# First convolution in nine block products, row sums by DMA, PSUM in pairs of banks

## The chip, the cores and the metric

The kernel runs on one core of a Trainium2 chip. The core has TensorE (PE; matmuls, with weight loads as PEld), VectorE (DVE), ScalarE (ACT) and GpSimd (POOL), and SyncE (SP), which here only issues DMAs. Each engine takes its instructions in order from its own queue. The metric is the device time of one execution in microseconds. The kernel before takes 885.22 us, the median of three runs (883.51 to 889.34).

## The reference

There are B = 4 images, C = 64 channels, and each (image, channel) is a 256 x 256 matrix, float32. Cut to what matters:

```python
# layer 0: per channel a separable filter k = hx (outer) hy, made by two small sine networks
k_f = rfft2(k, s=(512, 512)) / 512
u_f = rfft2(x, s=(512, 512))
y = irfft2(u_f * k_f, s=(512, 512))[..., :256, :256]     # a causal 2-D convolution
x = y + x * bias[:, None, None]
# layer 1
scores = einsum('bpsd,bptd->bpst', x, x) / sqrt(256)     # Gram matrix of the rows
red = sum(scores * weights[None], axis=-1, keepdims=True)
y = x + red                                              # one number per row s
y_hat = (y - mean) * rsqrt(var + 1e-5)                   # over images and positions, per channel
out = y_hat * gamma + beta
```

Because the filter is separable, the 2-D convolution is two products with lower triangular Toeplitz matrices of 256 x 256, one per side of the image.

## The kernel before

Each channel is worked on as a whole. Its four images lie as two pairs: u picks the half of the partitions (64 rows of the array) and v the other index. A 256 x 256 matrix is cut into blocks of 64, so that four 64 x 64 matmuls, t = 0 to 3, run beside each other on the four quarters of the array.

**TensorE, per channel, three stages.** `conv_x0` is the second convolution (from z, the result of the first, to x0); `conv_z` (lines 197 to 216) is the first convolution of the *next* channel; `gram` is the Gram matrix of x0. A Toeplitz matrix that is lower triangular has ten non-zero blocks out of sixteen, so a convolution has, for each of its four output block columns, products over 4, 3, 2 and 1 blocks: four matmuls with 256, 192, 128 and 64 moving columns. `gram` uses the symmetry and also has ten blocks.

**Around the stages.** `copy_z` (ScalarE) takes the first convolution out of PSUM, reversed. `add_bias` (VectorE, line 246) adds x times bias to the second one and writes x0. `weigh` (VectorE) multiplies the Gram blocks with the weights: two products with an accumulator give row sums (`red0`, lines 328), one product gives `pr` (line 319), whose columns are still to be summed over the partitions. `spread` (line 340) places the row sums on a diagonal and adds them to `pr`, giving `sp`. `all_sum` (GpSimd, line 348) sums `sp` over the partitions into `rd`, and `pick_red` (ScalarE, line 357) copies the second image's half. `add_red` (line 364) adds this to x0 and accumulates the sum for the mean; a small all-reduce on GpSimd (line 368) adds over partitions. `minus_mean` (line 411), `squares` (line 416), `sum_squares` (line 422, GpSimd), `root` (lines 428 to 432) and the Newton steps with scale and shift (lines 437 to 450, VectorE) make the normalisation, and `finish` (line 462, ScalarE) writes the output tile, which SP stores (line 463).

**Tables.** The filter values of all channels are written once to `g_dram`, four copies. `load_h` (line 188) loads a channel's Toeplitz rows into `toep` in four DMAs of 16 partitions, and `copy_h` (line 193, ScalarE) doubles them onto the other 64 partitions.

**The order** is written by hand: the program runs under a manual schedule, so each engine's queue, SP's and GpSimd's among them, has its instructions in the order in which the main loop writes them. One pass of that loop, for channel c, works on several channels at once: convolution and Gram of c, first convolution of c+1, loads for c+2 and c+3, row sums of p = c-1, mean and squares of q = c-2, scale and outputs of f = c-3 and e = c-4. The last two channels have their own code, `last_channels`, in which the row sums go through TensorE (`red_by_pe`). PSUM is used in eight single banks.

Of the kernel before, what the change touches and what calls it, by code (L numbers as in the profile page):

```python
# [16 lines left out]
P = 128  # L17
EMB = 33
FFT = 2 * S
GW = S + P // 2  # L20
COPIES = 4
H = P // 2
# [15 lines left out]
def conv_scores_bn_kernel(  # L38
# [29 lines left out]
    def load_xt(c, v, n):  # L68
        if not n:
            xts[c, v] = ld.tile([P, 4, S], F32, tag=f"xt{v}", name=f"xt_{c}_{v}", bufs=4)  # L70
        part = bass.ts(n, 2)
        nc.sync.dma_start(xts[c, v][:, part], xT[c, v, :, part])
# [39 lines left out]
    g_sb = const.tile([P, GW], F32, name="g_sb")  # L112
    nc.vector.memset(g_sb[:, S:], 0.0)

    g0_sb = const.tile([P, 2, GW], F32, name="g0_sb")
# [3 lines left out]

    g_dram = dram.tile([COPIES, C, 2, GW], F32, name="g_dram")  # L120

    hs[0] = ld.tile([P, 2, GW], F32, tag="toep", name="toep_0")
    with tc.tile_pool(name="fps", bufs=4, space=PSUM) as fps:
# [20 lines left out]
        for a in (1, 0):  # L144
# [7 lines left out]
            for n in range(2):  # L152
                row = g0_sb[H * n : H * n + 1, a, 32 * n :]
                src = bass.AP(row.tensor, row.offset, [row.ap[0], [1, 32], [1, S]])
                queue = nc.scalar if n else nc.sync
                queue.dma_start(hs[0][bass.ts(n, 32), a, :S], src)
# [5 lines left out]
        nc.vector.tensor_tensor(g_sb[:, :S], ph, decay_sb, ALU.mult)  # L162
        for a in (1, 0):
            nc.vector.tensor_copy(hs[0][H:, a, :S], hs[0][:H, a, :S])

# [3 lines left out]
    for a in (1, 0):  # L169
        queue = nc.scalar if a else nc.sync  # L170
        queue.dma_start(
            g_dram[:, :, a, :].rearrange("n c g -> c n g"),
            g_sb[bass.ts(a, C), None, :].to_broadcast([C, COPIES, GW]),
        )
# [3 lines left out]
    def load_h(c, n):  # L178


        if not n:
            hs[c] = ld.tile([P, 2, GW], F32, tag="toep", name=f"toep_{c}")
        src = bass.AP(
            g_dram.tensor, g_dram.offset + c * 2 * GW + 16 * n,
            [[4 + C * 2 * GW, COPIES], [1, 4], [1, GW + S]],
        )
        rows = hs[c][bass.ts(n, 16)].rearrange("p a r -> p (a r)")
        nc.sync.dma_start(rows[:, : GW + S], src)

    def copy_h(c):  # L190

        toep = hs[c]
        nc.scalar.copy(toep[H:, :, :S], toep[:H, :, :S])  # L193

    ps = ctx.enter_context(tc.tile_pool(name="ps", bufs=8, space=PSUM))

    st8, zs = {}, {}

    def conv_z(c, m):


        toep = hs[c]
        p1 = [ps.tile([P, 2, S], F32, tag="ps", name=f"p1_{c}_{m}_{u}") for u in range(2)]
        for k in range(2):
            for i in range(4):
                for t in range(4):
# [3 lines left out]
                        p1[u][bass.ts(v, H), k, : S - H * i],  # L212
                        lhsT=xts[c, v][rows, i, bass.ts(2 * m + k, H)],
                        rhs=toep[rows, 1, H * i : S], start=(i == 0), stop=(i == 3),
# [3 lines left out]
    def copy_z(c, m, p1):  # L218
        for u in range(2):
            nc.scalar.copy(zs[c][:, u, bass.ts(m, 2), :], p1[u][:, :, ::-1])  # L220

    def conv_x0(c, z, parts=range(2)):
# [3 lines left out]
        if not c:  # L226
            first_x0(z)
            return
        for m in parts:
            p2 = [ps.tile([P, 2, S], F32, tag="ps", name=f"p2_{c}_{m}_{v}") for v in range(2)]  # L230
            for i in range(2):
                for k in range(4):
                    for t in range(4):
                        v, u = t % 2, t // 2
                        rows = bass.ts(v, H)
                        nc.tensor.matmul(  # L236
                            p2[v][bass.ts(u, H), i, : S - H * k],
                            lhsT=z[rows, u, k, bass.ts(2 * m + i, H)],
                            rhs=toep[rows, 0, H * k : S], start=(k == 0), stop=(k == 3),
                        )  # L240
            add_bias(c, m, p2)

    def add_bias(c, m, p2):
        for v in range(2):
            part = bass.ts(m, 2)
            nc.vector.scalar_tensor_tensor(  # L246
                st8[c][0][:, v, part], xts[c, v][:, part], chan_sb[:, 0, c : c + 1],
                p2[v][:, :, ::-1], ALU.mult, ALU.add,
            )

    def first_x0(z):

        toep = hs[0]
        p2 = [
            [ps.tile([P, 2, S], F32, tag="ps", name=f"p2_0_{m}_{v}") for v in range(2)]
            for m in range(2)
        ]
        for half in range(2):
            for m in range(2):
                for i in range(2):  # L260
                    for k in range(2 * half, 2 * half + 2):
                        for t in range(4):
# [3 lines left out]
                                p2[m][v][bass.ts(u, H), i, : S - H * k],  # L266
                                lhsT=z[rows, u, k, bass.ts(2 * m + i, H)],
                                rhs=toep[rows, 0, H * k : S],
                                start=(i == 0 and k == 0), stop=(i == 1 and k == 3),
                            )  # L270
                if half:
                    add_bias(0, m, p2[m])

    def begin(c):
        x0 = wk.tile([P, 2, 4, S], F32, tag="x0", name=f"x0_{c}", bufs=5)
        red0 = sm.tile([P, B, 2], F32, tag="red0", name=f"red0_{c}")
# [7 lines left out]
    def gram(c, v, weighed=True):  # L284
# [3 lines left out]
        gs = [ps.tile([P, 8, H], F32, tag="ps", name=f"g_{c}_{v}_{u}") for u in range(2)]  # L288
# [15 lines left out]
        if not weighed:  # L304
            banks.extend(gs)
            return
        for u in range(2):
            weigh(c, 2 * v + u, gs[u])
        if c < BY_PE or (c == BY_PE and not v):
            for u in range(2):  # L310
                spread(c, 2 * v + u)

    def weigh(c, b, g, rows_last=True):

        _, red0, _, pr, _ = st8[c]
        w = ws[c]
# [465 lines left out]
```

## Time and profile before

| what | value |
|---|---|
| time, median of three runs | 885.22 us |
| span of the profiled execution | 872.5 us (the page gives no other time of this execution) |
| one channel in the steady part | 13.08 us |
| three TensorE stages, lines 211, 236, 299 | 304.0, 298.3 and 302.5 us busy |
| GpSimd all-reduce, line 348 | 62 times 6.08 us |
| spread, line 340 | 492 times 0.344 us, 139.0 us |
| bias addition, line 246 | 256 times 0.739 us, 173.8 us |
| DMA moved | 169.69 MB, 194 GB/s |

The page gives busy time by engine, the chain of work that ended last, and groups of equal instructions. A fp32 matmul is recorded as two passes, so 8192 records of a stage are 4096 matmuls. Four quarters of the array run at once and matmuls overlap, so the mean time of one (296 ns) is not the distance to the next. For VectorE and ScalarE too, the next instruction starts somewhat before the recorded end of the one before it; the distance from start to start is what an instruction holds its queue for. The granted TensorE clock is 0.994 of full speed in the mean.

### The profile page before, as it was taken

To read this page: it belongs to the slowest core of one execution; us is meant where nothing else is said; L and a number is where in the kernel's file an instruction comes from. 1 tells how busy PE (TensorE), PEld (TensorE's weight loads), DVE (VectorE), ACT (ScalarE), POOL (GpSimd) and SP (SyncE) were. 2 spreads that over 40 slices of the span, in tenths; PEclk is the share of its full clock that TensorE was granted. 3 is DMA by queue.
4 is the path that set the end of the run, shared out by engine and by line. 5 is a ranking of instruction groups with operands and counts; after the bars stand their busy time and mean duration, and the time that the engine had idled before them with its cause. 6 is when DMAs were issued, how large, how long until landed. Compare 5 with 4: busy or idle time off the path is not lost.

```text
span 872.5 us, 55963 instructions
## 1 busy us (share of the span) xinstructions
PE 855.9 (98%) x24674; PEld 836.2 (96%) x24674; DVE 755.9 (87%) x2647; ACT 621.9 (71%) x1218; POOL 427.8 (49%) x194
## 2 busy tenths in 40 slices
PE   7999999999999999999999999999999999999995
PEld 5999999999999999999999999999999999999994
DVE  3588988988988988988998998998998988988996
ACT  2256767767767767777777777777777767767786
POOL 0236546546546546546546546546546546546530
PEclk9999999999999999999999999999999999999997
DMA  6724665565565556565565565655555655565535
GB/s 189 221 77 139 198 209 195 201 211 193 201 210 192 200 196 206 202 207 193 203 208 192 203 206 194 205 200 199 203 201 199 202 203 192 204 210 193 190 141 194
DMA packets 89870, 169.69 MB, mean 194 GB/s; under 512 B 10555, under 2 KB 11740, under 8 KB 89628
## 3 DMA queue, kind: packets, MB, share of 16 engines
q1 hardware_dynamic: 88972, 165.52, 55.6%
q8 instruction: 194, 3.18, 1.6%
q10 hardware_dynamic: 656, 0.59, 0.3%
q14 instruction: 48, 0.39, 0.2%
HBM read 98.18 MB, written 67.76 MB: 190 GB/s over the span
## 4 chain that ended last, share of the span: by engine, by line
PE 97%; DVE 2%; DMA 1%; issue 0%; ACT 0%; DVEq 0%; ACTq 0%
PE p L211 32%; PE g L299 32%; PE p L236 32%; PE p L265 0%; DMA toep<-g_sb 0%; PE ph L132 0%; DVE junk L328 0%; DMA zw_sb<-in_zw 0%; PE rp L379 0%; DVE fa L135 0%; DVE x L516 0%; DVE pr L319 0%; PE rp L384 0%; PE s L507 0%; DVE fa L140 0%
## 5 line engine op out<-in xcount | busy, mean ns | idle before, releaser
L348 POOL PARTITION_ALL_REDUCE rd<-sp x62 | 376.8, 6078 | 182.4 <-DVE sp L340 182.4
L211 PE MATMUL p<-toep,xt 64*64 64x256 f32 (+3 forms) x8192 | 304.0, 296 | 0.9 <-DMA toep<-g_sb 0.9
L299 PE MATMUL g<-x 64*64 64x192 f32 (+1 forms) x8192 | 302.5, 296 | 0.0
L211 PEld LDWEIGHTS p<-toep,xt 64*64 64x64 f32 x8192 | 291.4, 133 | 8.6 <-PE idle L168 1.5
L236 PE MATMUL p<-toep,z 64*64 64x256 f32 (+3 forms) x8064 | 298.3, 296 | 0.0
L236 PEld LDWEIGHTS p<-toep,z 64*64 64x64 f32 x8064 | 289.6, 133 | 6.8 <-issue 0.2
L299 PEld LDWEIGHTS g<-x 64*64 64x64 f32 x8192 | 289.7, 133 | 0.8 <-DVE x L246 0.2
L328 DVE SCALAR_TENSOR_TENSOR junk<-g,w 128x192 f32<-128x192 f32 x512 | 160.9, 351 | 81.1 <-PE g L299 77.7
L462 ACT ACTIVATE o<-x,sh,g 128x512 f32<-128x512 f32 x252 | 203.3, 810 | 3.0
L246 DVE SCALAR_TENSOR_TENSOR x<-xt,chan_sb,p 128x512 f32<-128x512 f32 x256 | 173.8, 739 | 7.6 <-PE p L265 7.2
L220 ACT COPY z<-p 128x512 f32<-128x512 f32 x256 | 134.7, 576 | 22.3 <-PE p L211 22.3
L416 ACT ACTIVATE sq<-x,mom 128x1024 f32<-128x1024 f32 x127 | 145.2, 1143 | 3.3 <-DVE x L405 1.1
L364 DVE SCALAR_TENSOR_TENSOR x<-x,rd 128x1024 f32<-128x1024 f32 x122 | 144.1, 1218 | 0.0
L340 DVE SCALAR_TENSOR_TENSOR sp<-eye_sb,red,pr 128x128 f32<-128x128 f32 x492 | 139.0, 344 | 0.0
L368 POOL PARTITION_ALL_REDUCE mom<-mom x61 | 24.5, 401 | 231.1 <-DVE x L364 227.1
L357 ACT COPY rd<-rd 64x512 f32<-64x512 f32 (+1 forms) x62 | 38.0, 612 | 134.8 <-POOL rd L348 134.7
L319 DVE SCALAR_TENSOR_TENSOR pr<-g,w 128x256 f32<-128x256 f32 x256 | 107.3, 419 | 0.0
L193 ACT COPY toep<-toep 64x512 f32<-64x512 f32 x63 | 38.9, 617 | 32.0 <-DMA toep<-g_dram 26.7
L411 ACT ACTIVATE mom<-mom 128x1 f32<-128x1 f32 x62 | 18.2, 293 | 38.0 <-POOL mom L368 37.1
L328 DVE DVE_READ_ACCUMULATOR junk<-g,w 128x1 f32 x512 | 42.2, 82 | 0.0
L422 POOL PARTITION_ALL_REDUCE tot<-mom x62 | 29.8, 481 | 5.1 <-ACT sq L416 5.1
L416 ACT ACTIVATION_READ_ACCUMULATOR sq<-x,mom 128x1 f32 x127 | 23.7, 186 | 0.0
(84 smaller groups left out, 220.4 us busy)
## 6 DMA issues: line engine op xcount, KB each, us to landing
xt<-in_xT SPq DMA_DIRECT2D x256, 256.0 KB
out<-o SPq DMA_DIRECT2D x256, 256.0 KB
w<-in_wl SPq DMA_DIRECT2D x64, 320.0 KB
toep<-g_dram SPq DMA_DIRECT2D x252, 36.0 KB
g_dram<-g_sb SPq DMA_DIRECT2D x1, 320.0 KB
g_dram<-g_sb ACTq DMA_DIRECT2D x1, 320.0 KB
decay_sb<-in_decay SPq DMA_DIRECT2D x1, 256.0 KB
fw_sb<-in_fw ACTq DMA_DIRECT2D x1, 192.0 KB
```

The lines of the kernel that those rows point to most:

```text
L211: nc.tensor.matmul(p1[u][bass.ts(v, H), k, : S - H * i], lhsT=xts[c, v][rows, i, bass.ts(2 * m + k, H)], rhs=toep[rows, 1, H * i : S], sta ...
L220: nc.scalar.copy(zs[c][:, u, bass.ts(m, 2), :], p1[u][:, :, ::-1])
L236: nc.tensor.matmul(p2[v][bass.ts(u, H), i, : S - H * k], lhsT=z[rows, u, k, bass.ts(2 * m + i, H)], rhs=toep[rows, 0, H * k : S], start=(k ...
L246: nc.vector.scalar_tensor_tensor(st8[c][0][:, v, part], xts[c, v][:, part], chan_sb[:, 0, c : c + 1], p2[v][:, :, ::-1], ALU.mult, ALU.add,)
L299: nc.tensor.matmul(gs[u][bass.ts(h, H), o, :], lhsT=xb[rows, v, i, m, :], rhs=xb[rows, v, i, t, :], start=(i == 0), stop=(i == 3),)
L319: nc.vector.scalar_tensor_tensor(pr[:, b].rearrange("p (t s) -> p t s", s=H), g[:, COL, :], 1.0 / math.sqrt(S), w[:, 6:10, :], ALU.mult, A ...
L328: nc.vector.scalar_tensor_tensor(junk, g[:, part, :], 1.0 / math.sqrt(S), w[:, 3 * n : 3 * n + 3, :], ALU.mult, ALU.mult, accum_out=red0[: ...
L340: nc.vector.scalar_tensor_tensor(sp[:, b, part], eye_sb, red0[:, b, n : n + 1], pr[:, b, part], ALU.mult, ALU.add,)
L348: nc.gpsimd.partition_all_reduce(rd[:, part].rearrange("p b s -> p (b s)"), sp[:, part].rearrange("p b s -> p (b s)"), P, RED.add,)
L364: nc.vector.scalar_tensor_tensor(x0[:, v], x0[:, v], 1.0, rd[:, 2 * v, None, :].to_broadcast([P, 4, S]), ALU.mult, ALU.add, accum_out=mom[ ...
L416: nc.scalar.activation(sq, st8[c][0][:, v], AF.Square, bias=mom[:, 5:6], accum_out=mom[:, 6 + v : 7 + v])
L462: nc.scalar.activation(o, y, AF.Identity, bias=sh, scale=g)
```

## The change

**Nine blocks.** In the first convolution, blocks 1 and 2 of the input meet the same Toeplitz block in two places of the result. The new code forms their sum (`sums`, VectorE, 512 columns), multiplies it once with that block (`conv_shared`, four more matmul groups of 64 columns), and copies this to `kept` (ScalarE). The other products use *differences* of Toeplitz blocks, which lie ready in a longer `toep` (832 columns instead of 512), so that a group has 256, 128, 64 and 64 moving columns: with the shared one nine blocks. `copy_z` now copies half of the result, and `add_shared` (VectorE) adds `kept` to the other half while moving it. Channels 0, 1 and 63 keep the plain form.

**Row sums.** `spread` is gone from the main loop. `turn_rows` transposes the 32 columns that hold the row sums on VectorE and SP stores them to DRAM; `add_rows`, a DMA issued by GpSimd with an accumulating write, adds them to the first partition of `pr`; `all_sum` then reads `pr`. Both moved from the end of pass c to pass c+1.

**PSUM** is allocated in four pairs of banks, so that `add_bias` (in the main loop), `copy_z`, and the product of `weigh` handle both banks in one instruction. The scale steps are spread between other VectorE work, and several steps of the loop and of `last_channels` moved.

```diff
 def conv_shared(c):
+        for k in range(4):
+            for t in range(4):
+                nc.tensor.matmul(
+                    both[bass.ts(v, H), u, k], lhsT=xss[c][rows, v, bass.ts(k, H)],
+                    rhs=toep[rows, 11], start=(k == 0), stop=(k == 3),
+                )
+        nc.scalar.copy(kept[c]..., both[:, :, :4]...)
 def conv_z(c, m):
+            for i, (cols, outs) in enumerate((
+                (slice(9, 13), slice(0, 4)),
+                (slice(5, 13, 7), slice(0, 3, 2)),
+                (slice(7, 8), slice(1, 2)),
+                (slice(12, 13), slice(0, 1)),
+            )):
...
+    def turn_rows(c):
+        across = sm.tile([P, 32], F32, tag="across", name=f"across_{c}", bufs=2)
+        nc.vector.transpose(across, reds[c % 3])
+        rows[c] = dram.tile([P, 32], F32, name=f"rows_{c}")
+        nc.sync.dma_start(rows[c], across)
+    def add_rows(c):
+        pr = st8[c][3]
+        nc.gpsimd.dma_start(
+            pr[0:1].rearrange("p b (n q i) -> p (b n) q i", n=2, i=32),
+            rows.pop(c).rearrange("(q j) i -> j q i", q=4)[None, : 2 * B], accum_op=ALU.add,
+        )
...
 for c in range(C - 2):
+        parts_of(c, 0)
+        for n in range(2):
+            load_h(c + 2, n)
+        if c + 3 < C:
+            load_xt(c + 3, 0, 0)
+        ... p2 = conv_x0(c, z, 0)
+        parts_of(c, 1)
+        for n in range(2, 4):
+            load_h(c + 2, n)
+        if c + 3 < C:
+            load_xt(c + 3, 1, 0)
+        if f >= 0:
+            tot = sum_squares(f, moms[f])
+        if p >= 0:
+            turn_rows(p)
+            add_rows(p)
+        ... add_bias(c, 0, p2); pick_red(q); scales[f] = root(f, tot)
+        for v in range(2):
+            if q >= 0:
+                add_red(q, v)
+            next(steps, None)
+        if q >= 0:
+            sum_means(moms[q])
+        if p >= 0:
+            all_sum(p)
+        if c + 2 < C - 1:
+            sums(c + 2)
+        ... p2 = conv_x0(c, z, 1); parts_of(c, 2); loads; add_bias(c, 1, p2); scale steps
+        if short:
+            conv_shared(c + 1)
+        if q >= 0:
+            minus_mean(moms[q])
+        for m in range(2):
+            if short:
+                p1 = conv_z(c + 1, m)
+                copy_z(c + 1, m, p1)
+                add_shared(c + 1, m, p1)
+            ...
+            if q >= 0:
+                squares(q, moms[q], m)
+        copy_h(c + 2)
+        parts_of(c, 3)
+        if c + 3 < C:
+            load_xt(c + 3, 1, 1)
+        parts_of(c, 4)
+        gram(c, 0)
+        gram(c, 1)
```

`parts_of(c, 0)` to `(c, 3)` are one `finish` each: second half of the first pair and both halves of the second pair of channel e, then the first half of channel f.

## The prediction

> **What bounds the kernel now.** I read the page's engine totals and its chain first, then one steady stretch, the waits, and the order of time inside one channel. The totals and the shares of the chain:
>
> ```profile
> PE 855.9 (98%) x24674; PEld 836.2 (96%) x24674; DVE 755.9 (87%) x2647; ACT 621.9 (71%) x1218; POOL 427.8 (49%) x194
> ...
> PE 97%; DVE 2%; DMA 1%; issue 0%; ACT 0%; DVEq 0%; ACTq 0%
> ```
>
> TensorE never stops, and the chain is TensorE. The starts of the first convolution in the chain (103.48, 116.56, 129.64 us) lie 13.08 us apart: one channel. The table of stretches for one such channel:
>
> ```profile
> 440.00:453.08 13.08, 13.08 (x395) 12.89 (x389) 11.71 (x42) 9.72 (x19) 6.92 (x3) 1.00 0.59 201
> ```
>
> PE 13.08 busy, VectorE 11.71, ScalarE 9.72, GpSimd 6.92, clock 1.00. So TensorE sets 13.08; VectorE has 1.4 us to spare, ScalarE 3.4, GpSimd 6.2. From the waits:
>
> ```profile
> ACT mom L411 <- POOL mom L368: 37.1, 51, 5.6
> ...
> PEld g L299 <- DVE x L246: 0.2, 1, 0.2
> ```
>
> and from SP's own:
>
> ```profile
> SPq L463 <- ACT o L462: 211.8, 175, 4.9
> ```
>
> ScalarE waits a little for GpSimd's sum of means, TensorE for nobody, and SP's DMA queue waits for ScalarE before each store: what stands behind a store is as late as ScalarE is. In order of time:
>
> ```profile
> 442.21 0.34 SPq L463 DMA_DIRECT2D out<-o  x1
> ...
> 442.44 0.40 POOL L368 PARTITION_ALL_REDUCE mom<-mom  x1 [3.73 <-DVE x L364]
> ...
> 442.61 0.43 SPq L72 DMA_DIRECT2D xt<-in_xT  x1
> ...
> 442.87 0.29 ACT L411 ACTIVATE mom<-mom 128x1 f32<-128x1 f32 x1 [0.68 <-POOL mom L368]
> ...
> 443.13 0.63 SPq L188 DMA_DIRECT2D toep<-g_dram  x1
> ...
> 443.43 1.15 ACT L416 ACTIVATE sq<-x,mom 128x1024 f32<-128x1024 f32 x1
> ...
> 444.58 0.80 ACT L462 ACTIVATE o<-x,sh,g 128x512 f32<-128x512 f32 x1
> ...
> 445.29 1.13 ACT L416 ACTIVATE sq<-x,mom 128x1024 f32<-128x1024 f32 x1
> ...
> 446.42 1.04 ACT L220 COPY z<-p 128x512 f32<-128x512 f32 x2
> ...
> 447.36 0.82 ACT L462 ACTIVATE o<-x,sh,g 128x512 f32<-128x512 f32 x1
> ```
>
> Start to start gives what each holds its queue: both means 0.56, a square 1.15, a copy of z 0.47, a finish 0.71 (0.81 until its data is there); on SP a store 0.40, an xt load 0.50, a toep load 0.67 (0.63 and a wait).
>
> **The change, part by part.** *Nine blocks.* The convolution's stage takes 4.37 us in the chain for ten 64-column blocks; nine are 3.93, so 0.44 goes and TensorE needs 12.64 us in a channel (61 channels have it: 26.8 us). The mean matmul times 217, 269, 323, 377 ns for 64 to 256 columns rise by 53 per 64, so a small block costs its share if it can be issued. The start times in the trace around 23.06 us, where only 128- and 64-column matmuls run, show 48 in a row at 20.9 ns each and no gap; the new channel needs 12.64 us for 416 of them, 30 ns each. I take the full saving. The Trainium skill, "TensorE: Matmul & The Clock Gate", section "Wait — 56ns, not 53.3ns?", speaks against it: start to start of matmuls never drops below about 25 ns. The 20.9 ns row contradicts that; by the rule the 24 passes of 64 columns in a channel would cost 100 ns for four tiles instead of 54, which eats the saving.
>
> *VectorE.* Out: eight spreads, 2.1 us (four from 443.97 to 445.02). Merged: four bias additions of 0.66 become two of 1.19, four products of 0.33 two of 0.60, saving 0.4. New: the sum of two xt blocks and two additions of the shared part, 512 elements each, 0.60 by the products' rate (256 elements in 0.33, 1.04 ns an element): 1.8. The transpose is in no row; between a memset's 0.06 and a spread's 0.34 I take 0.15, as it handles 32 columns. The five scale steps go between long ones; 1.34 or less. Sum: 11.4 against 11.9, inside 12.64. If TensorE set the pace, the second bias addition would end about 0.3 us before gram needs it: thin cover, and 0.1 us over it costs 6 us.
>
> *ScalarE.* Two z copies fewer and one for the shared part, -0.5; copying the longer toep +0.27 (832 columns for 512; copies of 256 and 512 take 402 and 617 ns, so 0.84 ns a column): no load gained. *PSUM pairs.* The same bytes; each pair is needed again four allocations later, and the tightest (gram's first, after the second bias addition) waits for that anyway: nothing. *Toep loads* grow from 36 to 52 KB, 4 MB in all against 169.69: nothing.
>
> *Row sums by DMA.* Here I see the cost. Per channel a transposed tile is stored by SP, and GpSimd then issues an adding DMA that must wait until that store has landed. GpSimd works in order: behind the waiting issue stand this channel's sum of means and its all-reduce. For the sum of means ScalarE waits (minus_mean), and behind minus_mean stand both z copies, both squares, the toep copy, and the two finishes whose stores SP waits for. SP has the new store behind the second of these stores. So the queues close to a ring, once round per channel:
>
> - ScalarE: means 0.56, z copy 0.50, square 1.15, z copy 0.50, square 1.15, toep copy 0.90, finish 0.71, finish 0.81 until its data: 6.28
> - SP: store 0.40, two toep 1.34, xt 0.50, store 0.40, two toep 1.34, xt 0.50: 4.48
> - the row store until it has landed: 2.65
> - GpSimd: waking 0.17 (442.27 to 442.44), the DMA's issue 0.63, the sum 0.40; waking ScalarE 0.05: 1.25
>
> Together 14.66 us, more than TensorE's 12.64 and than today's 13.08. Today there is no ring: GpSimd's sum waits for VectorE alone.
>
> Two terms are in no row. The landing: the landing marks give 1.85 us for the first load on an idle queue, 2.65 for toep loads, up to 3.8 for xt loads; the new one is a small transfer behind loads, like toep, so 2.65. GpSimd's issue of a DMA: between its own shortest instruction (0.10) and the longest single issue on SP (1.05, a store); a pattern of three steps like toep's, so 0.63. Ends: 13.33 and 16.23. By the skill ("DMA: Bandwidth & Descriptors", "Specifications", first byte about 1 µs on the gpsimd path) the issue may be 1.0 if that is spent in it, the ring 15.03 and the total 21 us more; no row shows it.
>
> The adding DMA's landing (2.65 too, up to 3.8) precedes the all-reduce, whose result is due a channel later: from issue to issue there are 14.66 us, and issue and landing 3.28, all-reduce 6.12, copy of its result 0.72 with waking, two additions into x0 2.5 make 12.6. Two us are left, at 3.8 one. So 0.
>
> *Start and end.* Two subtractions of 0.23 in the start, ahead of channel 1's tables, not channel 0's; the end is re-ordered around the same matmuls, entered with ScalarE late. I count 0, give or take 5.
>
> **Sum.** Stores start with channel 4, so some five channels run at 12.64 (-2.2), then 56 at 14.66: 56 x 1.58 = +88.5. In all +86. The profiled execution's span is 872.5; the page has no other time of it, and the median shown, 885.2, lies 12.7 above, which I take as what surrounds the span. 872.5 + 86 + 12.7 = 971.5; I say **972 us**.
>
> **The rivals.**
> - *Faster, 860 us:* the ring doesn't bind and nine blocks pay in full, 61 x 0.42 (12.64 and a seam against 13.08) = 25.6 off. One mechanism decides: the row store leaves SP early enough for GpSimd's issue to come before the sum of means is ready. It holds if landing and issue together take under 1.3 us, or if SP isn't held by the stores. For: VectorE has the rows ready 2 us into the channel, and SP is idle much of its time. Against: no landing under 1.85, and the 211.8 us of stores waiting. 0.08.
> - *The same, 888:* every term of the ring at its least (landing 1.85, issue 0.10, toep 0.63): 13.17, and 56 x 0.09 - 2 = +3, 888. The saving is just given back. 0.06.
> - *Much slower, 1060 and up:* issue 1.05 and landing 3.8 make 16.23: 56 x 3.15 - 2 = +174, 1059; issue of 2 us 17.2, 1113. For: the new store is behind 1.2 MB of stores and loads issued in 4.5 us, and DMA is 59% busy today. 0.16.
> - *Forecast, ring of 13.4 to 16:* 0.70.
>
> **Numbers.** A change of 1% (9 us) is about what a measurement of this kernel can tell from no change. The ring's lower end, 13.33, gives 56 x 0.25 - 2 = +12, 897; its upper end 1059. With the end's 5 us the range is 892 to 1060: below lie the first two rivals (0.14), above some 0.05. Faster 0.08, same 0.06, slower 0.86.
>
> **What would show it.** In the profile after: convolution starts 14 to 16 us apart; PE near 85% with idle before the second convolution (z late) or gram (x0 late); ScalarE's L411-like means waiting 3 us or more in each channel for GpSimd's sum; GpSimd idle some 5 us before its DMA, released by the row store's landing; that store leaving SP straight behind an xt load. VectorE near 78%. Wrong if starts lie 12.7 apart: then the store went out earlier than the written order says, or issue and landing are far shorter than any row. If they lie apart by more than 16.3, the issue or landing is beyond its upper row.

## The result, and the profile after

The changed kernel takes **1143.91 us** (median of four, 1141.62 to 1144.94) against 884.37 us for the kernel before in the same comparison: a ratio of **1.2931, 95% interval 1.2883 to 1.2978**. The forecast was 972 us with a range that ended at 1060. The direction and the place were right, the size was not.

The engine totals, the chain by engine and by line (shares of the span), and the queue that brings instructions (packets, MB, share of 16 DMA engines), from the page of the changed kernel:

```profile
PE 929.4 (82%) x26626; PEld 808.3 (71%) x26626; DVE 713.6 (63%) x2160; ACT 603.3 (53%) x1157; POOL 481.9 (42%) x255
...
q8 instruction: 209, 3.42, 1.3%
...
DMA 35%; POOL 20%; ACT 14%; DVE 10%; issue 8%; PE 7%; SPq 5%; POOLq 0%; DVEq 0%; ACTq 0%
DMA rows<-across 19%; POOL rd L457 17%; DMA pr<-rows 8%; ACT sq L526 4%; DMA xt<-in_xT 4%; SPq L203 3%; ACT o L590 3%; PE p L313 3%; PE g L380 2%; DVE x L473 2%; ACT rd L466 2%; POOL pr L447 2%; DVE x L329 2%; DVE junk L406 2%; DMA toep<-g_dram 2%
```

The chain was 97% TensorE and is now 7%. No engine has taken its place: the largest share of a single line is a transfer of 16 KB, `rows<-across`, the store of the transposed row sums. The granted TensorE clock is 0.951 in the mean, against 0.994 before; with TensorE at 7% of the chain this is not what the time is lost by, and in the stretch shown below it is 1.00. The waits (us in all, times, longest):

```profile
POOL pr L447 <- DMA rows<-across: 528.0, 60, 40.3
ACT mom L521 <- POOL mom L479: 433.5, 62, 9.2
DVE z L277 <- ACT z L271: 366.7, 121, 7.0
PEld p L313 <- DVE z L277: 98.5, 51, 3.8
PEld g L380 <- DVE x L329: 96.6, 56, 3.4
```

and those of SP's queue:

```profile
SPq L591 <- ACT o L590: 559.3, 91, 10.2
```

From the second to the fourth, each line waits for work that stands behind the line above it in a queue: GpSimd's adding DMA waits for the row store, ScalarE's mean for GpSimd's sum behind that DMA, VectorE's part of z for ScalarE's copy behind the mean, and TensorE for z. (The fifth line is TensorE's wait for x0.) SP's output stores, which are ahead of the row store in SP's queue, wait for ScalarE's finishes. From the row store over GpSimd, ScalarE and SP back to the next row store this is a closed ring, and the order of time shows one turn of it (start, length, engine and line; in brackets the idle time before and what ended it):

```profile
559.98 0.89 POOL L447 DMA_DIRECT2D pr<-rows  x1 [8.78 <-DMA rows<-across]
560.60 0.65 POOL L479 PARTITION_ALL_REDUCE mom<-mom  x1
561.28 0.29 ACT L521 ACTIVATE mom<-mom 128x1 f32<-128x1 f32 x1 [7.82 <-POOL mom L479]
...
562.32 0.69 DVE L277 TENSOR_TENSOR z<-p,kept 128x512 f32<-128x512 f32 x1 [5.86 <-ACT z L271]
...
565.97 2.22 ACT L590 ACTIVATE o<-x,sh,g 128x512 f32<-128x512 f32 x3
566.81 0.34 SPq L591 DMA_DIRECT2D out<-o  x1
...
567.73 0.40 SPq L591 DMA_DIRECT2D out<-o  x1
568.23 1.28 SPq L203 DMA_DIRECT2D toep<-g_dram  x2
...
569.86 0.80 ACT L590 ACTIVATE o<-x,sh,g 128x512 f32<-128x512 f32 x1
...
570.09 1.49 SPq L591 DMA_DIRECT2D out<-o  x1
...
571.63 1.28 SPq L203 DMA_DIRECT2D toep<-g_dram  x2
572.96 0.44 SPq L76 DMA_DIRECT2D xt<-in_xT  x1
573.51 0.37 SPq L442 DMA_DIRECT2D rows<-across  x1
...
578.28 0.89 POOL L447 DMA_DIRECT2D pr<-rows  x1 [9.42 <-DMA rows<-across]
```

The page's chain also runs through the all-reduce (`POOL rd L457`, 17%) and the landing of the adding DMA (`DMA pr<-rows`, 8%), which are not in the ring. It gets there, in another turn, by putting the last output store ahead of the row store, issued at 343.48, down to a finish behind the all-reduce that ends at 343.53. By the code that store belongs to the finish before; and in the turn above, too, it is issued at 570.09, while the later finish, begun at 569.86, ends only at 570.66. This part of the chain is inferred, and the order of time does not bear it out.

From one adding DMA to the next 18.30 us pass. In that stretch (busy us and instructions of PE, PEld, DVE, ACT and POOL, then clock, DMA share, GB/s) the engines do what they did in 13.08 us before:

```profile
559.98:578.28 18.30, 14.28 (x444) 12.37 (x432) 10.93 (x33) 9.40 (x18) 7.78 (x4) 1.00 0.47 145
```

Over the steady part one turn is 17.66 us in the mean. The starts of the second convolution of channels 1 to 5 lie 12.8 to 13.8 us apart, the next ones 16.3 and more: the ring sets in when SP has stores to wait for.

### The profile page after: what moved, and what is told of

It is laid out like the page before. It is cut to its first block, busy times and chain, and to the rows that moved or that the text cites. A ratio compares the mean times of both kernels' runs of the same rounds, so it can differ in the third digit from the quotient of the medians.

```text
span 1139.5 us, 59137 instructions
## 1 busy us (share of the span) xinstructions
PE 929.4 (82%) x26626; PEld 808.3 (71%) x26626; DVE 713.6 (63%) x2160; ACT 603.3 (53%) x1157; POOL 481.9 (42%) x255
## 4 chain that ended last, share of the span: by engine, by line
DMA 35%; POOL 20%; ACT 14%; DVE 10%; issue 8%; PE 7%; SPq 5%; POOLq 0%; DVEq 0%; ACTq 0%
DMA rows<-across 19%; POOL rd L457 17%; DMA pr<-rows 8%; ACT sq L526 4%; DMA xt<-in_xT 4%; SPq L203 3%; ACT o L590 3%; PE p L313 3%; PE g L380 2%; DVE x L473 2%; ACT rd L466 2%; POOL pr L447 2%; DVE x L329 2%; DVE junk L406 2%; DMA toep<-g_dram 2%
## 5 line engine op out<-in xcount | busy, mean ns | idle before, releaser
L457 POOL PARTITION_ALL_REDUCE rd<-pr x61 | 373.4, 6122 | 91.3 <-DMA pr<-rows 91.3
L277 DVE TENSOR_TENSOR z<-p,kept 128x512 f32<-128x512 f32 x122 | 84.3, 691 | 366.7 <-ACT z L271 366.7
L447 POOL DMA_DIRECT2D pr<-rows x61 | 54.2, 888 | 530.4 <-DMA rows<-across 528.0
L521 ACT ACTIVATE mom<-mom 128x1 f32<-128x1 f32 x62 | 18.3, 295 | 433.5 <-POOL mom L479 433.5
L262 PE MATMUL p<-toep,xt 64*64 64x64 f32 (+2 forms) x7808 | 235.8, 272 | 14.0 <-issue 14.0
L262 PEld LDWEIGHTS p<-toep,xt 64*64 64x64 f32 x7808 | 206.3, 134 | 38.9 <-issue 18.0
L329 DVE SCALAR_TENSOR_TENSOR x<-xt,chan_sb,p 128x1024 f32<-128x1024 f32 x122 | 153.4, 1258 | 1.3 <-PE p L313 1.3
L395 DVE SCALAR_TENSOR_TENSOR pr<-g,w 128x512 f32<-128x512 f32 x126 | 86.6, 688 | 0.0
L271 ACT COPY z<-p 128x512 f32<-128x512 f32 x122 | 69.5, 570 | 2.6 <-PE p L262 2.6
L208 ACT COPY toep<-toep 64x832 f32<-64x832 f32 x63 | 55.7, 884 | 7.3 <-DMA toep<-g_dram 5.7
L225 DVE TENSOR_TENSOR xs<-xt 128x512 f32<-128x512 f32 x61 | 41.6, 683 | 6.3 <-DMA xt<-in_xT 5.7
```

The costliest lines, as they stand in the source:

```text
L262: nc.tensor.matmul(out[:, outs], lhsT=xts[c][rows, v, i, bass.ts(2 * m + k, H)], rhs=toep[rows, cols], start=(i == 0), stop=(i == 3),)
L277: nc.vector.tensor_tensor(z[:, :, :1:-1, ::-1], y[:, :, :2], part[:, :, None, :].to_broadcast([P, 4, 2, H]), ALU.add,)
L329: nc.vector.scalar_tensor_tensor(st8[c][0][:, :, part], xts[c][:, :, part], chan_sb[:, 0, c : c + 1], p2[:, :, :, ::-1], ALU.mult, ALU.add,)
L395: nc.vector.scalar_tensor_tensor(pr[:, 2 * v : 2 * v + 2].rearrange("p u (t s) -> p u t s", s=H), both[:, :, COL, :], 1.0 / math.sqrt(S), ...
L447: nc.gpsimd.dma_start(pr[0:1].rearrange("p b (n q i) -> p (b n) q i", n=2, i=32), rows.pop(c).rearrange("(q j) i -> j q i", q=4)[None, : 2 ...
L457: nc.gpsimd.partition_all_reduce(rd[:, part].rearrange("p b s -> p (b s)"), sp[:, part].rearrange("p b s -> p (b s)"), P, RED.add,)
```

## The experiments

For each run the time is the median of four executions (of ten for the new order of loads in the kernel before), with the ratio to the kernel before and its interval. Where no ratio stands, the time is that of a single execution. The kernel before took between 881.0 and 882.5 us in the medians of these comparisons. "Period" is the mean distance of GpSimd's sums of means (the small all-reduce) in the steady part, 13.09 us before and 17.66 after.

### Is it the ring?

**One more square on ScalarE, inside the ring.** Between the mean and the first copy of z, 1.15 us:

```diff
         if q >= 0:
             minus_mean(moms[q])
+            extra = wk.tile([P, 4, S], F32, tag="sq", name=f"extra_{c}", bufs=1)
+            nc.scalar.activation(extra, st8[q][0][:, 0], AF.Square, bias=moms[q][:, 5:6])
```

> ScalarE computes one more square of 1024 columns (its result is not used) between minus_mean and the copy of z, 1.15 us in each channel from 2 on. Ring theory: every microsecond put on the ring is paid in full, 17.66 becomes 18.8 us a channel, time 1144 + 57 x 1.15 = 1205 to 1220 us, though ScalarE is only 53% busy. Rival (ScalarE's wait for GpSimd is slack behind something else): within 1% of 1144 us.

Measured: 1202.27 us, just under the expected band: 58.4 us more, 1.02 for each of 57 channels, where 1.15 were added; period 18.68. ScalarE's part of the ring grew from 6.21 to 7.39 us, the rest of it became a little shorter. ScalarE was busy 53% of the span, and still nine tenths of what is added to it are paid: it is in the ring.

**The sum of means ahead of the adding DMA** in GpSimd's queue:

```diff
-            add_rows(p)
...
         if q >= 0:
             sum_means(moms[q])
+        if p >= 0:
+            add_rows(p)
```

> On GpSimd the sum of means goes ahead of the adding DMA; the row store keeps its place on SP. Ring theory: ScalarE no longer waits for the row store, the ring over one channel is cut; what is left is a longer path over two channels (row store 4.5, adding DMA issue and landing 3.1, all-reduce 6.1, copy 0.8, two additions and the sum 3.2, ScalarE 6.2, SP 5.6: 29.5 us in two periods, 14.7 each), so 960 to 990 us. Rival A (the landing of the row store itself is what costs): little change, above 1100 us. Rival that only the order of the sum of means matters: below 890 us.

Measured: 996.8 us, period 15.08, 7 us above the expected band and far from both rivals. 147 us go when the waiting DMA no longer stands ahead of the sum. What is late next is the all-reduce behind the DMA, by which ScalarE's copy of its result waits 231.3 us in all.

**The row store at the head of the pass**, ahead of the output stores and loads that held it back:

```diff
         z = zs.pop(c)
+        if p >= 0:
+            turn_rows(p)
         parts_of(c, 0)
...
         if p >= 0:
-            turn_rows(p)
             add_rows(p)
```

> The transposed row sums are stored first in each pass of the loop, ahead of the two output stores and their loads on SP; nothing else differs from the changed kernel. Ring theory (the row store stands behind output stores that wait for ScalarE, ScalarE waits for the sum of means, which stands behind the adding DMA, which waits for the row store): the 5.6 us on SP and the ScalarE part leave the ring, TensorE or VectorE set the pace, 12.7 to 13.1 us a channel instead of 17.66, time 862 to 885 us. Rival A (the row store is slow in itself, 128 pieces of 128 bytes into DRAM, 4.5 us to land wherever it is issued, and this is what costs): the time stays above 1000 us. Rival B (pairs of banks or small matmuls cost the time): unchanged, about 1140 us.

**The whole row-sum traffic left out**, so that the result lacks the row sums of channels 0 to 60:

```diff
-        if p >= 0:
-            turn_rows(p)
-            add_rows(p)
```

> The transpose, the row store and the adding DMA are left out, so the row-sum part of the scores of channels 0 to 60 is not in the result; all else as in the changed kernel. Ring theory: 12.7 us a channel, 860 to 875 us; this is what nine blocks and pairs of banks are worth without any row-sum traffic. Rival B (nine blocks or pairs of banks cost the time): above 950 us.

Measured: 936.46 us with the early store (ratio 1.0626, 1.0571 to 1.0681; period 14.11) and 955.92 us with no traffic at all (period 14.49). One moved call takes 207 us away: the ring is what the changed kernel lost most by. But both stay far above the 860 to 885 that was expected with the ring gone, and the kernel that does *less* is the slower of the two, by 2% in its one execution. A second limit lay under the first. In the early-store kernel it shows in the chain by engine:

```profile
PE 82%; issue 6%; DVE 4%; DMA 4%; POOL 2%; ACT 1%; SPq 0%; DVEq 0%; POOLq 0%; ACTq 0%
```

and in the waits:

```profile
PEld g L380 <- issue: 40.7, 50, 2.0
...
PEld p L262 <- issue: 24.4, 32, 1.8
```

TensorE stands with nothing to wait for that the profile knows. Before, the chain had 0% of that.

**The row store issued by GpSimd**, just ahead of its own adding DMA, so that SP has no part in it:

```diff
-        nc.sync.dma_start(rows[c], across)
+        nc.gpsimd.dma_start(rows[c], across)
```

> One word: the row store is issued by GpSimd, just ahead of the adding DMA that waits for it, instead of by SP. The same transfer, the same wait ahead of the sum of the means; but the store no longer stands behind SP's output stores and loads. Ring theory: the ring needs SP's place in it, so it falls apart and only the fetch loss is left: 925 to 960 (GpSimd still waits for the landing, 2.5 to 4 us, ahead of the sum). Rival (the wait on a landing ahead of the sum of the means costs the time, wherever the store is issued): 1080 or more.

Measured: 1003.73 us, period 15.22, between the two theories. Taking SP out does open the ring (140 us less), but GpSimd's own queue is then the limit, as its order of time shows:

```profile
497.89 6.12 POOL L457 PARTITION_ALL_REDUCE rd<-pr  x1 [3.50 <-DMA pr<-rows]
503.93 0.48 POOL L532 PARTITION_ALL_REDUCE tot<-mom  x1
504.28 0.59 POOL L442 DMA_DIRECT2D rows<-across  x1
510.43 0.87 POOL L447 DMA_DIRECT2D pr<-rows  x1 [5.56 <-DMA rows<-across]
511.06 0.62 POOL L479 PARTITION_ALL_REDUCE mom<-mom  x1
513.51 6.12 POOL L457 PARTITION_ALL_REDUCE rd<-pr  x1 [1.83 <-DMA pr<-rows]
```

Two landings are waited for (5.56 and 1.83 us here), and with 6.12 of all-reduce and the short instructions one round is 15.6 us. An engine that issues a DMA and waits for it is not busy, and can still be full.

### What is the second limit?

The gaps marked "issue" have a place. If TensorE's matmuls and weight loads, and the few semaphore instructions of its queue between them, are numbered together in the order of their starts (the first is number 0), then in the run without row sums 82 of the 89 distances of over 0.25 us between two starts from 30 us on end at number 193 or a multiple of 256 after it, 92.4 of their 105.0 us. The packets of the queue named "instruction" are 16,384 bytes each, and there are 194 of them before and 209 after, for 49,680 and 53,523 instructions numbered like this: one packet for 256 instructions. The table takes from each trace, for these boundaries, the time lost in all (what the gap between two starts there has over 0.05 us), the time in which 256 instructions pass without the gap, and how long after a boundary its packet starts (means over the steady part; the first packet goes with the first boundary, and so on).

| kernel | us | lost at boundaries, us | 256 instructions last, us | packet starts after, us |
|---|---|---|---|---|
| before | 881 to 885 | 0.8 | 4.32 | 0.68 |
| after | 1143.91 | 18.6 | 5.28 | 0.95 |
| early store, nine blocks | 936.46 | 70.4 | 3.92 | 1.60 |
| no row sums, nine blocks | 955.92 | 90.5 | 3.93 | 1.57 |
| no row sums, ten blocks | 935.93 | 52.8 | 4.33 | 1.83 |
| early store, ten blocks | 906.02 | 21.6 | 4.36 | 1.39 |
| before, matmuls cut at 128 | 981.75 | 80.5 | 3.80 | 1.55 |

936.5 - 70.4 and 955.9 - 90.5 are 866 and 865 us: without the gaps both would be where the ring's removal should have brought them. In the early-store kernel a packet takes 1.23 us in the mean, and where TensorE lost over 0.2 us it went on a median 1.38 us after the end of the packet that started at the boundary before. With 1.60 until it starts these make some 4.2 us from boundary to boundary, more than the 3.9 that 256 instructions last.

**Ten blocks again, no row sums:**

```diff
-        short = c + 1 > 1
+        short = False
...
-        if c + 2 < C - 1:
-            sums(c + 2)
```

> The first convolution goes back to its ten products of whole blocks for every channel, and the row-sum traffic (transpose, row store, adding DMA) is left out as in the run without row sums, so the row-sum part is missing in the result. Theory (the nine-block stage uses TensorE's instructions up faster than they are fetched: the run without row sums lost 90.5 us at the boundaries of 256 instructions): ten blocks issue fewer and longer matmuls, so the boundaries cost under 5 us again and the time is 880 to 895, 60 to 75 us below the 956 of the nine-block version without row sums. Rival (the changed order of SP's loads, two at once, delays the fetch whatever TensorE does): the boundaries still cost 40 us or more and the time stays above 920.

Measured: 935.93 us, 52.8 us lost. This is on the rival's side. But fewer instructions did save 38 of the 90.5 us at the boundaries, so both could have a part; the next runs take one at a time.

**More instructions, nothing else.** The kernel before, with the first convolution's products cut at 128 columns:

```diff
-                    nc.tensor.matmul(
-                        p1[u][bass.ts(v, H), k, : S - H * i], ...
-                        rhs=toep[rows, 1, H * i : S], start=(i == 0), stop=(i == 3),
-                    )
+                    for j in range(0, S - H * i, P):
+                        wide = min(P, S - H * i - j)
+                        nc.tensor.matmul(
+                            p1[u][bass.ts(v, H), k, j : j + wide], ...
+                            rhs=toep[rows, 1, H * i + j :][:, :wide],
+                            start=(i == 0 and j == 0), stop=(i == 3),
+                        )
```

> The kernel before with nothing changed but the first convolution's products cut at 128 columns: 256 becomes 128 and 128, 192 becomes 128 and 64. The same columns and the same loads, but 384 TensorE instructions in that stage of 4.3 us instead of 256, so 256 of them last 2.9 us. Theory (a fetch comes 3.2 us or more after the one before, so denser instructions wait for it): 0.3 to 0.75 us lost at 1.5 boundaries per channel, 30 to 70 us in all, 912 to 955. Rival (only the changed DMA traffic makes the fetch late, the number of instructions does nothing): boundaries under 5 us, 880 to 890.

Measured: 981.75 us against 881.0. The loads, their order and the columns are those of the kernel before; the packets are now 226:

```profile
q8 instruction: 226, 3.70, 1.7%
```

and TensorE waits in the stage that was cut and in the one after it:

```profile
PEld p L213 <- issue: 47.2, 63, 2.5
...
PEld g L302 <- issue: 27.3, 35, 1.6
```

80.5 us of the 100.7 are lost at the boundaries, more than expected. Most of the rest is the stage itself: outside of the boundaries its 384 instructions start 12.31 ns apart, 4.73 us, where 256 took 17.37 ns, 4.45 us; 0.28 us in some 62 channels are 17. So dense instructions alone bring the second limit about. With them the packets start later as well, 1.55 us after the boundary instead of 0.68, though the loads are unchanged.

**Which part of the DMA traffic?** Four runs change the loads.

Ten blocks with the early store:

```diff
-        short = c + 1 > 1
+        short = False
...
+        if p >= 0:
+            turn_rows(p)
         parts_of(c, 0)
```

> The row store at the head of the pass, and the first convolution in ten whole blocks for every channel; row sums are turned and added by DMA and PSUM goes in pairs of banks as in the changed kernel. Theory (the ring is cut by the early row store; the second loss is that of the nine-block stage's instruction fetch): 880 to 900, boundaries under 8 us, no more than 2 per cent from the kernel before. Rival (the ring's DMAs or SP's order cost by themselves): above 920, about the 936 of the nine-block version.

Measured: 906.02 us, ratio 1.0256 (1.0193 to 1.0319), 21.6 us lost: 30 us less than with nine blocks, and near the expected band without being in it.

The Toeplitz loads one at a time instead of two, nine blocks, early store (whose lines are left out here):

```diff
-        for n in range(2):
-            load_h(c + 2, n)
+        load_h(c + 2, 0)
...
-        for n in range(2, 4):
-            load_h(c + 2, n)
+        load_h(c + 2, 1)
...
+        load_h(c + 2, 2)
         load_w(c + 1)
+        load_h(c + 2, 3)
```

> The row store at the head of the pass as in the earlier run (936 us, 70.4 us lost at the instruction boundaries), and the four loads of the Toeplitz matrix are issued one by one over the pass instead of two by two. Theory of dense instructions: no large change, 920 to 945, the boundaries still lose 50 us or more. Rival (bunched loads stand in the way of the instruction fetch): the boundaries lose less than 20 us and the time is 870 to 890.

Measured: 954.3 us, the median of three executions, ratio 1.08 (1.0723 to 1.0878); a fourth, of which the trace is, took 962.48. Worse than with two at a time, and above both bands. In the trace some 85 us are lost at the boundaries, where the rival had under 20: two loads at once are not what alone makes the packets late. That it is slower still may come from the last load, now so late that ScalarE's copy of the Toeplitz matrix waits for it, 58.7 us in all.

Ten blocks, early store, and rows of 576 columns as the kernel before loads them (it copies 512 of these). Of the edit only the line that sets the width is shown:

```diff
-PLAIN = DIFFS + S
+PLAIN = DIFFS
```

> The ten-block version with the early row store (906 us, 21.6 us lost at TensorE's boundaries of 256 instructions), with the Toeplitz rows loaded 576 columns wide as in the kernel before, not 832: the differences that ten blocks don't need are no longer stored and loaded, 66 KB less per channel. Everything else, SP's order too, stays. Theory (the fetch of TensorE's instructions waits behind the kernel's own loads, and the wider rows are what makes it late): boundaries under 8 us, 882 to 893. Rival (SP's order, two loads at once, or the small transfers of the row sums make it late): boundaries still over 15 us, 898 to 908.

Measured: 913.56 us, ratio 1.0339 (1.0289 to 1.039), 36.2 us lost. This is the rival's side, and somewhat beyond it: the wide rows are not the cause.

SP's order of loads, from both sides. First the new order alone, in the kernel before:

```diff
-        if c + 2 < C and c:
-            load_xt(c + 2, 1, 1)
-        load_h(c + 2, 0)
+        for n in range(2):
+            load_h(c + 2, n)
+        if c + 3 < C:
+            load_xt(c + 3, 0, 0)
...
+        for n in range(2, 4):
+            load_h(c + 2, n)
         if c + 3 < C:
-            load_xt(c + 3, 0, 0)
-        load_h(c + 2, 1)
+            load_xt(c + 3, 1, 0)
...
```

> The kernel before with nothing changed but the order in which SP issues its loads: two Toeplitz loads and one of the input at the head of the pass, two and one in the second place, the weights and one, and one, as in the changed kernel. Theory (the new order of the loads makes the instruction fetch late): 15 us or more lost at the boundaries of 256 instructions, 895 to 925. Rival (the order alone does nothing; what makes the fetch late is the freer running of the other queues, or many small causes): boundaries under 5 us, 878 to 890.

Measured: 885.16 us, ratio 1.003 (1.0002 to 1.0059), 12.3 us lost at the boundaries: the rival's time, and a loss between the two. Then the old order (and the old place of the copy of the Toeplitz matrix) in the narrow ten-block kernel; for the loads this is the edit above the other way round.

> The ten-block version with early row store and narrow Toeplitz rows (914 us, 36 us lost at the boundaries), with SP's loads and the copy of the Toeplitz matrix back in the order of the kernel before. Theory (order): boundaries under 10 us, 880 to 895. Rival (not the order): boundaries still over 20 us, 900 to 920.

Measured: 890.77 us, ratio 1.0103 (1.0043 to 1.0163), 10.5 us lost instead of 36.2, about where the theory had them. So the order has a part at the boundaries: some 12 us alone, some 26 us in the second run, there together with the place of the copy, which was not tried by itself. It hardly moves the time of the kernel before. What remains to 882 us in this version is 8 us, less than the 10.5 that its boundaries still lose.

**Can nine blocks pay?** Early store and narrow rows, with the two blocks of differences that are used subtracted on VectorE. First in the middle of the pass, then at its head (only the new function is shown; `toep` gets room for its results):

```diff
+    def diffs(c):
+        toep = hs[c].rearrange("p (b s) -> p b s", s=H)
+        nc.vector.tensor_tensor(
+            toep[:, 0:11:10], toep[:, 7:10:2],
+            toep[:, 8:9].to_broadcast([P, 2, H]), ALU.subtract,
+        )
```

> Nine blocks and the early row store (936 us, 70.4 us lost at the boundaries), with the Toeplitz rows loaded 576 columns wide as in the kernel before; the two blocks of differences that the nine products use are subtracted on VectorE (one instruction of 128 x 128 per channel, about 0.3 us). Theory (dense instructions and wide rows both take part): the boundaries lose 15 to 35 us, 875 to 900. Rival A (only dense instructions count): 925 to 940. Rival B (only the wide rows count): boundaries under 8 us, 862 to 872, faster than before.

Measured: 987.53 us, ratio 1.1206 (1.1178 to 1.1233), only 15.2 us lost at the boundaries. None of the theories: the subtraction stood behind longer work on VectorE, and TensorE waited for it instead of for instructions:

```profile
PEld p L265 <- DVE toep L208: 125.6, 60, 3.4
```

> Nine blocks with narrow Toeplitz rows and the differences subtracted on VectorE at the head of the pass instead of in its middle, where TensorE waited 126 us for them (987 us). Fetch theory: those waits go, and with them the time in which the fetches caught up: the boundaries lose 40 to 90 us instead of 15, and the time is 915 to 950, about the 936 of nine blocks with wide rows. Rival (the waits were the whole cost, the fetch keeps up): boundaries under 20 us, 865 to 885.

Measured: 934.35 us, ratio 1.0625 (1.0546 to 1.0705), 70.5 us lost, as the fetch theory had it. The wait for VectorE went and the wait for instructions came back to what it was:

```profile
PEld g L383 <- issue: 40.1, 45, 2.3
...
PEld p L265 <- issue: 25.1, 33, 2.0
```

None of the versions is faster than the kernel before. If the loss at the boundaries is taken off the execution that each trace shows, the versions with the ten-block stage as it was come to 875 to 885 us, and the nine-block ones that neither the ring nor another wait holds (early store, no row sums, loads one by one, differences at the head) to 862 to 877. This is a subtraction, not a run: by it nine blocks would be worth some 10 us against ten if the instructions came in time.

## Why the prediction was wrong

**What bounds the kernel, and the ring: right.** The forecast named the four queues, their order and the channel from which it holds. Cutting it at either of its two ends (early store, sum ahead of the DMA) took 207 and 147 us away, and a dose in its ScalarE part was paid for nine tenths.

**The sum of the ring: two terms too small.** This is the step that failed. The parts that the forecast added, and their means in the trace after:

| part of the ring | forecast, us | measured, us |
|---|---|---|
| row store issued, until GpSimd issues the adding DMA | 2.65 + 0.17 | 4.53 |
| SP, from the finish to the row store | 4.48 | 5.62 |
| adding DMA's issue | 0.63 | 0.62 |
| sum of means and waking ScalarE | 0.45 | 0.68 |
| ScalarE, mean to second finish | 6.28 | 6.21 |
| turn | 14.66 | 17.66 |

The first row is 1.71 us too small. Of this 1.29 are the landing: taken as 2.65 "behind loads, like toep" with 3.8 as the upper end, it has a mean of 3.94 and goes from 3.1 to 5.3 in the steady part. The other 0.42 are GpSimd's waking: 0.59 us from the last landing mark to the issue, where 0.17, the waking behind a VectorE instruction, was taken. The upper end, 3.8, is the longest landing of an xt load in the stretch of before that the forecast read (430 to 458 us). Over the steady part of that trace xt loads take up to 5.2, and a quarter of the toep loads 3.3 us or more, so the upper end was too low already. The traffic changed too, and other landings rose: xt loads from a median of 3.30 to 4.19, output stores 2.63 to 3.64, toep loads 2.73 to 4.25. SP's part had no upper bound in the forecast: what each DMA holds SP's queue for was read from one stretch of before as if it were a fixed cost, though in the steady part of that trace one xt load in ten held it for 1.17 us or more. In the turn shown above a store holds it 1.49 us where one took 0.34 to 0.40; of the 1.14 us that SP's part is longer, 0.47 lie ahead of the first of these stores and 0.67 in the two store-to-store steps. With the other rows this makes 3.00 us too few in a turn, and 56 turns make 168 us of the 172 by which the forecast was short.

**GpSimd's issue of a DMA: right.** It holds the queue for 0.62 us (0.63 was taken). The Trainium skill, "DMA: Bandwidth & Descriptors", section "Specifications", gives a first-byte latency of about 1 µs for the gpsimd path. The queue does not pay that here: the record is 0.89 us long, and the sum of means starts 0.62 after the record's start.

**Nine blocks, "I take the full saving": wrong, and hidden by the ring.** The condition in the forecast's own sentence, "if it can be issued", did not hold. The instructions that do the work with fewer columns are more, and TensorE's instructions arrive in packets too slowly for them: with the ring cut, 70 us are lost where 26.8 were to be gained. The 48 passes at 20.9 ns on which the forecast rested are, with as many weight loads, 96 instructions, fewer than one packet brings, so they could not show this. In the changed kernel only 18.6 us are lost this way: TensorE waits for z and x0 there, and 256 instructions last 5.28 us. Outside of the boundaries the stage does become shorter: 320 instructions 12.9 ns apart, 4.13 us, against 4.45 before, 0.32 of the 0.44. The rule weighed in the forecast, from the Trainium skill, "TensorE: Matmul & The Clock Gate", section "Wait — 56ns, not 53.3ns?", that matmuls never start less than about 25 ns apart, is contradicted, for four matmuls side by side on the quarters of the array, by the early-store kernel too: where eight or more 64-column passes follow each other (257 rows of them without a boundary inside), a pass takes 16.3 ns in the mean, from the first start of the row to the first start behind it. So the rule came out on the right side of the saving for a reason that has nothing to do with it.

**The base: 10 us too high.** The 12.7 us taken as surrounding the span were probably for the most part an execution that happened to be faster than the median. The profiled execution after took 1141.62 us with a span of 1139.5: 2.1 us lie around it. The early-store kernel's has 1.7. This error went the other way and hid part of the first: without it the forecast would have been short by some 183 us, of which some 15 are not assigned to any term.

**The rivals.** The ring did bind, so "faster" and "the same" fell. "Much slower" was the nearest, and had the landing at 3.8; but it got its time from GpSimd's issue at 1.05, which was 0.62, and not from SP. "Faster, 860" described what lies behind the ring if instructions came in time: 936.5 - 70.4 = 866.

**The smaller terms.** VectorE is busy 713.6 us, 11.5 for each of 62 channels (11.4 forecast), though its merged and new instructions of 512 elements take 0.68 to 0.69 us, not 0.60; the transpose takes 0.20 us (0.15). Of "what would show it": the row store does leave SP straight behind an xt load, GpSimd does wait for its landing, 8.8 us rather than 5, ScalarE's mean waits 433.5 / 62 = 7.0 us (3 or more), PE is at 82% (85), VectorE at 63% (78). The starts are 17.66 us apart, beyond the 16.3 at which the forecast said that the landing or the issue must lie beyond its upper row: it was the landing with GpSimd's waking, and SP. The pairs of banks were not tried by themselves; they are in the ten-block version at 890.77 us, so they and all else in it cost no more than 1.6%.

## What to carry to other kernels

When a change makes an engine wait for a DMA's landing, follow the queue behind the waiting instruction until it comes back to the DMA that is waited for; if it does, the time of a round is the sum over all queues, whatever each engine's share of busy time is. Size the transfers in such a sum with room above: landings and a DMA queue's holding times belong to the traffic, not to the instruction, and a change moves the traffic. And when a change gives TensorE fewer columns in more instructions, compare the time that 256 of its instructions last with the time in which the next packet of them arrives.

## What the hardware did unexpectedly

TensorE's instructions come by DMA, 256 at a time, and a packet of them mostly starts some time after TensorE has passed the boundary before. In the run without row sums this time goes with the kernel's own traffic: of its 158 boundaries from 150 to 850 us, those in whose next 1.5 us the other queues used under half of the 16 DMA engines' time saw the packet start after 1.15 us in the mean (63 boundaries), and those with 0.9 or more after 2.28 (29); the correlation is 0.56. It is a correlation; that the packet queues behind the loads was not tried by itself. In the kernel before a packet had ended a median 2.55 us before TensorE came to it, and never less than 1.33. TensorE waited for none of them for more than 0.2 us, with one exception. Where it did wait, in all these kernels, the median from the packet's end until it went on is 1.35 to 1.5 us in each of them. So the kernel before ran within about a microsecond of a limit that no busy share shows, and the versions with the old instruction count and other DMA traffic lose 10 to 53 us by it.

What starts a packet is open. In the steady part before, 23 of 175 packets start ahead of the first instruction behind their boundary, by up to 0.2 us, and after, where TensorE waits for z and x0, 24 of 189 by up to 1.2. So it is not the execution of that instruction; that the boundary is passed earlier in TensorE's queue would fit, but no run here tests it. In the early-store kernel late packets do not come in series: a boundary loses time in 48% of the cases behind one that did, and in 45% behind one that did not.
